# A 1 MB load cut into 8 runs and 24 runs in a kernel whose DMA engines are always busy

## The chip, the cores and the metric

The kernel runs on one core of a Trainium2 chip. A core has five engines that run their own instruction streams: PE (matrix products), ACT and DVE (element-wise work), POOL, and SP, which here only issues transfers. Sixteen DMA engines move data between the device memory and the core's 128-partition memory. The metric is the device time of one execution in microseconds; the runs of the kernel before have a median of 323.83 us.

## The reference

`x` is 128 batches of 128 channels by 1024 time steps in float32 (67.1 MB). Each batch has a subject number, which picks one of eight 128 x 128 weight matrices. The output is `x` plus the product of the picked matrix, transposed, with `x`:

```python
w = weights[subjects]
out = jnp.einsum('bct,bcd->bdt', x, w)
x = x + out
```

All of `x` is read once and an output of the same size is written once.

## The kernel before

A tile is four batches, 2 MB. There are 32 tiles (`NT`), and 12 slots (`SLOTS`) of 16 KB a partition hold them; tile i lies in slot i mod 12. The result replaces the input in its slot and is stored from there.

*Loads.* `load` (L142) issues two transfers of 1 MB for a tile, both on ACT's queue, one for each pair of batches (`H` = 2 pairs of `G` = 2). A transfer reads 32 runs of eight rows, 32 KB each and contiguous in device memory, and puts two rows into each of 128 partitions, so a run fills four partitions with 8 KB each: the first batch of a pair lies in partitions 0 to 63, the second in 64 to 127. Each transfer adds 16 to the semaphore `s_in` of its tile's place modulo 4 when it is complete. Four tiles (`AHEAD`) are loaded ahead before anything else on ACT (L263). After that ACT's loop (L268) waits for a tile (`landed`, L154: 32 on its semaphore), waits for a free slot (`s_empty`, which POOL raises as stores complete), issues the load four tiles on, and then calls `trade` for the tile that has landed.

*Trade.* Two halves of partitions are exchanged by five copies on ACT (`move`, L152), so that each batch has its two rows of a channel pair where the product needs them. `trade` ends with `s_ready`.

*Product.* For each pair, DVE places four weight matrices with the identity added (`place`, L192), so that the product contains the `+ x`; PE multiplies them with the slot's rows in pieces of 512 columns (L204); DVE copies the result from the accumulators into the slot (L216) and raises `s_added`. Before the first tile DVE and POOL rearrange the eight weight matrices, and eight dummy products run on PE.

*Stores.* SP waits for `s_added` and issues stores: the first 20 tiles one by one with 2 MB each, the last 12 in pairs of 4 MB. The first one is issued at L306, the others through `transfer` (L66), which ACT's loads use too. The program ends when the last store has landed.

## Time and profile before

| | |
|---|---|
| runs, median (lowest to highest) | 323.83 us (323.4 to 324.35) |
| profiled execution, its own time | 323.66 us |
| its span, first to last instruction | 321.7 us |
| bytes read, written | 67.63 MB, 67.11 MB |
| mean rate over the span | 419 GB/s |
| PE, ACT, DVE busy | 77%, 61%, 56% |
| loads of x: number, size, median to landing | 64, 1024 KB, 11.6 us |
| stores of 2 MB: number, median to landing | 20, 52.1 us |
| stores of 4 MB: number, median to landing | 6, 32.3 us |

The page cuts the span into 40 slices of 8 us. A digit is the busy share in tenths, and the DMA row is the mean of the 16 DMA engines. A DMA queue is a list of transfers of one issuing engine; both queues are worked on by the same 16 engines. A packet is what one engine moves in one piece, or the small write by which it reports that its part is complete. Packets are counted in the stretch in which they start, so that a short stretch can show a share above 1. In a row of windows the columns are the stretch, its length, busy time and count of instructions of PE, its weight loads, DVE, ACT and POOL, then the clock that PE was granted, the DMA share and GB/s.

### The profile page before, as it was taken

What the parts mean: (1) busy time and instruction counts of PE and PEld (TensorE: products, weight loads), DVE (VectorE), ACT (ScalarE), POOL (GpSimd) and SP (SyncE); (2) the same over time, 40 slices, a digit from 0 to 9 for tenths busy, and PEclk for the clock granted to TensorE, in tenths of its full rate; (3) what the DMA queues carried; (4) which work ended last, traced back from release to release, by engine and by line L of the source; (5) the groups of instructions that cost most, each with busy time, mean ns of one, the idle gap of its engine ahead of it and who ended that gap; (6) DMA issues with size and microseconds to landing.
All of it is one profiled execution on the core that took longest, in us unless ns stands there. A gap on an engine that the chain in (4) does not pass through costs nothing. (4 is left out here: it accounts for less than half of the span.)

```text
span 321.7 us, 2843 instructions
## 1 busy us (share of the span) xinstructions
PE 247.7 (77%) x528; PEld 102.2 (32%) x528; DVE 181.4 (56%) x217; ACT 195.7 (61%) x162; POOL 2.5 (1%) x10
## 2 busy tenths in 40 slices
PE   7479987888888888888793998749787589999200
PEld 3134332333333333333341433313333234444000
DVE  3707765666666665666275276544743666677500
ACT  1577767776777677775627766377662799990000
POOL 0200000000000000000000000000000000000000
PEclk9969999999999999999798699998997999999955
DMA  8999999999999999999999999999999999999994
GB/s 318 399 456 440 401 418 403 432 438 432 424 454 403 436 418 442 436 436 426 405 428 434 424 420 438 418 434 434 416 442 418 448 405 432 428 434 432 428 428 200
DMA packets 7731, 134.76 MB, mean 419 GB/s; under 512 B 1457, under 2 KB 1458, under 8 KB 2098
## 3 DMA queue, kind: packets, MB, share of 16 engines
q1 hardware_dynamic: 4658, 67.64, 49.7%
q10 hardware_dynamic: 3072, 67.11, 48.9%
q14 instruction: 1, 0.01, 0.0%
HBM read 67.63 MB, written 67.11 MB: 419 GB/s over the span
## 5 line engine op out<-in xcount | busy, mean ns | idle before, releaser
L204 PE MATMUL ps<-x_all,w 128*128 x512 | 237.5, 618 | 50.1 <-PEq L200 49.5
L216 DVE COPY x_all<-ps 128x2048 f32 x64 | 146.7, 2292 | 114.8 <-DVEq L215 114.8
L204 PEld LDWEIGHTS ps<-x_all,w 128*128 128x128 f32 x512 | 98.2, 197 | 189.5 <-issue 189.5
L152 ACT COPY aside<-x_all 64x1024 f32 (+1 forms) x64 | 66.7, 1042 | 76.9 <-issue 75.1
L152 ACT COPY x_all<-aside 64x1024 f32 (+1 forms) x64 | 66.8, 1044 | 4.7
L152 ACT COPY x_all<-x_all (+1 forms) x32 | 60.7, 1897 | 6.2 <-ACTq L162 5.7
L192 DVE TENSOR_TENSOR w<-w_all,eye 128x128 f32<-128x128 f32 x132 | 31.8, 283 | 0.8 <-issue 0.8
L228 PE MATMUL ps<-x_all 128*128 128x512 f32 x16 | 10.2, 808 | 1.7 <-DVE x_all L225 1.7
L228 PEld LDWEIGHTS ps<-x_all 128*128 128x128 f32 x16 | 4.1, 262 | 7.0 <-issue 5.3
L266 ACT ACT_TABLE_LOAD x1 | 1.3, 1283 | 6.2 <-issue 6.2
L286 DVE COPY w_all<-x_all 32x256 f32<-32x256 f32 x12 | 3.9, 327 | 0.4
L237 DVE STREAM_TRANSPOSE x_all<-x_all 128x512 f32<-128x512 f32 x2 | 2.0, 1082 | 3.0 <-DMA x_all<-in_L_cond_weights_dram 3.0
L286 POOL COPY w_all<-x_all 32x256 f32<-32x256 f32 x4 | 1.7, 427 | 7.0 <-DVE x_all L283 6.8
L283 DVE STREAM_TRANSPOSE x_all<-x_all 128x1024 f32<-128x1024 f32 x1 | 1.2, 1225 | 0.0
L225 DVE MEMSET x_all<- 128x512 f32 x1 | 0.5, 485 | 1.0 <-SPq L218 1.0
L243 DVE TENSOR_SCALAR x_all<-x_all 1x128 int32<-1x128 int32 x1 | 0.2, 215 | 0.7 <-DMA x_all<-in_itok_B_dram 0.7
L253 POOL TENSOR_SCALAR_AFFINE_SELECT eye<-x_all 128x128 f32<-128x128 f32 x1 | 0.3, 294 | 1.4 <-DVE x_all L225 1.4
L247 DVE CUSTOM_DVE_ANT_0 index<-x_all 1x256 uint16<-1x256 uint16 x1 | 0.3, 280 | 0.0
L253 POOL TENSOR_SCALAR_AFFINE_SELECT eye<-eye 128x128 f32<-128x128 f32 x1 | 0.3, 294 | 0.1
L245 DVE TENSOR_SCALAR x_all<-x_all 1x128 int32<-1x128 int32 x1 | 0.2, 216 | 0.0
L266 ACT COPY mark<-eye 1x1 f32<-1x1 f32 x1 | 0.2, 190 | 0.0
L353 POOL MEMSET const-bfloat16-1.0<- 128x1 bf16 x1 | 0.1, 101 | 0.0
(5 smaller groups left out, 0.4 us busy)
## 6 DMA issues: line engine op xcount, KB each, us to landing
x_all<-in_x_dram ACTq DMA_DIRECT2D x64, 1024.0 KB, 11.6
out_dram<-x_all SPq DMA_DIRECT2D x20, 2048.0 KB, 52.1
out_dram<-x_all SPq DMA_DIRECT2D x6, 4096.0 KB, 32.3
x_all<-in_L_cond_weights_dram SPq DMA_DIRECT2D x1, 512.0 KB, 3.7
x_all<-in_itok_B_dram SPq DMA_DIRECT2D x1, 0.5 KB
```

The source lines that it names most:

```text
L152: return nc.scalar.copy(out, in_)
L192: copy = nc.vector.tensor_tensor(ws[q], w_all[:, bass.ds(subject[q], 1), :], eye, ALU.add)
L204: mm = nc.tensor.matmul(ps[h][:, q % G, t : t + N], ws[q][:, 0, :], x_all[:, bass.ds(at, N)], start=True, stop=True,)
L216: nc.vector.tensor_copy(mine, ps[h].rearrange("d g t -> d (g t)")).then_inc(s_added, 1)
L225: nc.vector.memset(zeros, 0.0).then_inc(s_zeros, 1)
L228: nc.tensor.matmul(ps[P_SLOTS - 1][:, G - 1, :N], zeros[:, :D], zeros, start=True, stop=True)
L237: nc.vector.transpose(w_mid.rearrange("p (e r h w j) -> p r j h e w", e=4, r=R, h=4, w=8)[:, r], w_raw.rearrange("p (j r d) -> p r j d", r ...
L247: nc.vector.tensor_tensor(index[:, :B], near, wrap, ALU.add).then_inc(s_index, 1)
L253: nc.gpsimd.affine_select(eye[:, 0], eye[:, 0] if r else zeros[:, :D], [[-1, D]], ALU.not_equal, 1.0, base=r - r * R * A, channel_multipli ...
L266: nc.scalar.copy(mark, eye[:1, 0, :1]).then_inc(s_moved, H)
L283: nc.vector.transpose(w_late, w_mid).then_inc(s_sort, 1)
L286: engine.tensor_copy(w_all[32 * v : 32 * (v + 1), 2 * o : 2 * (o + 1), :], w_late[32 * o : 32 * (o + 1)].rearrange("c (e u r d) -> c u r e ...
```

## The change

The second transfer of tile 0, batches 2 and 3 into slot 0, is issued as two transfers: first the last 8 of its 32 runs, into partitions 96 to 127, then the other 24, into partitions 0 to 95. The first of them reports to a semaphore of its own, `s_cut`; the second to `s_in[0]` as before. ACT waits for `s_cut` once, ahead of its loop. All other loads are issued as before.

```diff
+CUT = 24
...
+    s_cut = tc.alloc_semaphore("s_cut")
...
-    def load(k, slot, first):
+    def load(k, slot, first, cut=None):
         for h in range(H):
-            transfer(
-                nc,
-                nc.scalar,
-                x_all[:, bass.ds(slot * (H * G * T) + h * G * T, G * T)],
-                x[bass.ds(first + h * G, G)].rearrange("h (b r) t -> (h b) (r t)", r=ROWS),
-            ).then_inc(s_in[k], DMA)
+            there = x_all[:, bass.ds(slot * (H * G * T) + h * G * T, G * T)]
+            runs = x[bass.ds(first + h * G, G)].rearrange("h (b r) t -> (h b) (r t)", r=ROWS)
+            if cut and h:
+                rows = cut * ROWS // R
+                transfer(nc, nc.scalar, there[rows:], runs[cut:]).then_inc(s_cut, DMA)
+                there, runs = there[:rows], runs[:cut]
+            transfer(nc, nc.scalar, there, runs).then_inc(s_in[k], DMA)
...
         for i in range(AHEAD):
-            load(i % AHEAD, i, i * (H * G))
+            load(i % AHEAD, i, i * (H * G), None if i else CUT)
         nc.scalar.wait_ge(s_eye, R)
         nc.scalar.copy(mark, eye[:1, 0, :1]).then_inc(s_moved, H)
         nc.gpsimd.wait_ge(s_eye, R).then_inc(s_empty, SLOTS - 1 - AHEAD)
+        nc.scalar.wait_ge(s_cut, DMA)
         with nc.scalar.Fori(0, NT // AHEAD - 1) as turn:
```

## The prediction

> **What bounds the kernel now.** I read the page's slices first, because 134.76 MB pass through one core and the busiest compute engine is idle for a quarter of the span:

> ```profile
> PE 247.7 (77%) x528; PEld 102.2 (32%) x528; DVE 181.4 (56%) x217; ACT 195.7 (61%) x162; POOL 2.5 (1%) x10
> DMA  8999999999999999999999999999999999999994
> DMA packets 7731, 134.76 MB, mean 419 GB/s; under 512 B 1457, under 2 KB 1458, under 8 KB 2098
> q1 hardware_dynamic: 4658, 67.64, 49.7%
> q10 hardware_dynamic: 3072, 67.11, 48.9%
> ```

> The 16 DMA engines are busy in every slice but the first and the last, and the two queues (q10 holds the loads, q1 the stores and the two small inputs) add up to 98.6% of 16 engines' span. No compute engine comes near that. Next the view of SP's waits and the windows, for the middle and for the end:

> ```profile
> SPq L362 <- DMA out_dram<-x_all: 17.4, 1, 17.4
> 60.00:300.00 240.00, 200.36 (x432) 82.72 (x432) 145.33 (x163) 158.33 (x131) 0.00 (x0) 0.96 1.01 429
> 302.50:316.00 13.50, 0.00 (x0) 0.00 (x0) 0.00 (x0) 0.00 (x0) 0.00 (x0) 0.59 1.00 427
> ```

> From 60 to 300 us the DMA share is 1.01 (packets are counted where they start) at 429 GB/s, and after 302.5 nothing computes: the rest is stores draining, and the program's end waits 17.4 us for them. The chain of waits stops at the last compute work and does not show this tail. So the time is the time of the DMA engine that ends last, and the question is which engine that is and how much work it has. The DMA view of four short stretches at the end answers the first half (each fence line is that stretch's count; stretches 316.0 to 317.0, 317.0 to 318.7, 318.7 to 319.5, 319.5 to 321.7):

> ```profile
> DMA packets 16, 0.52 MB, mean 524 GB/s; under 512 B 0, under 2 KB 0, under 8 KB 0
> ...
> DMA packets 16, 0.07 MB, mean 39 GB/s; under 512 B 14, under 2 KB 14, under 8 KB 14
> ...
> DMA packets 2, 0.03 MB, mean 41 GB/s; under 512 B 1, under 2 KB 1, under 8 KB 1
> ...
> DMA packets 1, 0.00 MB, mean 0 GB/s; under 512 B 1, under 2 KB 1, under 8 KB 1
> ```

> The packets under 512 B are completion marks, one for each engine of a transfer (the count is checked below). Fourteen engines post the mark of the last store before 318.7, one between 318.7 and 319.5, and the last one after 319.5: it started its final 32 KB piece in the third stretch, alone. One engine thus ends about 2 us behind the bulk of the others, although by packets all 16 have had the same bytes. The page does not say which of the 16 it is.

> **The change part by part.**

> (1) *Work by engine.* q10 has 3072 packets for 64 loads, 48 each: 32 runs of 32 KB and 16 marks. Check: 64 and 26 transfers of 16 marks, 16 for the weights and one for the 512 B of indices are 1024 + 416 + 16 + 1 = 1457, the number under 512 B. So a load of 32 runs occupies 16 engines with two runs each, and a transfer of one run occupies one engine. The time of a run on its engine is 48.9% of 321.7 us x 16 engines / 2048 runs = 1.23 us. For the 8 runs and the 24 runs no row exists. The bounds: if the chip cut both pieces evenly over all 16 engines, every engine would keep its 64 KB and this part is 0; if the pieces are dealt in whole runs and begin at the same engine, some engines get 3 runs where they had 2, others 0. I take the second, because the rows (32 runs to 16 engines, one run to one) fit whole runs dealt over as many engines as divide their number, which is 8 engines with one run each and then 12 with two each: 8 engines get three runs (+1.23 us), 4 keep two (0), 4 get none (-2.46 us).

> [...]

> (2) *Is the added work covered?* Nothing hides it. All engines have queued work from the first load to the end: reads alone move at 430 GB/s and then mixed traffic keeps the share of 1.01, so an engine with 1.23 us more work early ends 1.23 us later, and one with less ends earlier.

> ```profile
> 6.84:9.28 2.44, 2.44 (x6) 1.10 (x5) 1.83 (x4) 0.84 (x2) 0.00 (x0) 1.00 1.00 430
> 9.28:11.72 2.44, 2.44 (x6) 0.78 (x5) 2.25 (x7) 0.17 (x1) 1.71 (x4) 1.00 1.00 430
> ```

> Whether the time follows depends on whether the engine that ends last is one of the 8. By count alone that is 8 in 16. But if it is among the 4 unchanged or the 4 relieved, the 8 heavier ones of the other fifteen still end 1.23 us later, so a relief wins little (below). I take it among the 8.

> (3) *Sharing of partitions.* [...] If the way into a group of partitions is no wider than one engine, two engines that meet there halve. Bounds: 0, and all three shifted runs of a heavy engine at half speed, 3 x 1.23 = 3.7 us. No row shows two engines on one group. I take one run's worth, 1.2 us, since runs that collide drift apart as soon as one engine is ahead.

> [...]

> (4) *Two more instructions on ACT.* One more DMA issue, and a wait on the 8 runs ahead of the loop. In the rows of the order below (ACT's start, with the two pieces as 32 and 96 partitions) the loads sit ahead of everything else on ACT.

> ```order
> L66 DMA x_all<-in_x_dram 128x2048 x8
> L266 ACT_TABLE_LOAD [waits s_eye]
> L266 COPY mark<-eye 1x1
> L268 UNCONDITIONAL_BRANCH
> L64 ISA [waits s_in0,s_empty]
> ```

> ```order
> L68 DMA x_all<-in_x_dram 128x2048
> L68 DMA x_all<-in_x_dram 32x2048
> L68 DMA x_all<-in_x_dram 96x2048
> L68 DMA x_all<-in_x_dram 128x2048 x6
> L270 ACT_TABLE_LOAD [waits s_eye]
> L270 COPY mark<-eye 1x1
> L273 UNCONDITIONAL_BRANCH [waits s_cut]
> L66 ISA [waits s_in0,s_empty]
> ```

> Eight transfers became nine, with the new wait in front of the loop that already waits for slot 0. The timeline of ACT prices it:

> ```profile
> 0.90 5.21 ACTq L66 DMA_DIRECT2D x_all<-in_x_dram  x8
> 6.20 1.28 ACT L266 ACT_TABLE_LOAD   x1 [6.20 <-issue]
> 7.50 0.19 ACT L266 COPY mark<-eye 1x1 f32<-1x1 f32 x1
> 10.22 1.16 ACTq L66 DMA_DIRECT2D x_all<-in_x_dram  x2
> 11.55 2.11 ACT L152 COPY aside<-x_all 64x1024 f32 x2 [3.86 <-issue]
> 18.45 1.15 ACTq L66 DMA_DIRECT2D x_all<-in_x_dram  x2
> 26.66 1.15 ACTq L66 DMA_DIRECT2D x_all<-in_x_dram  x2
> ```

> An issue takes 5.21 / 8 = 0.65 us; it lies in the gap between 7.69, when the mark is made, and 10.22, when slot 0 has landed. The queue stays full, for a load takes 2.44 us to move and 0.65 to issue. Cost 0. The new wait adds nothing to the wait for slot 0; behind it stand the issues of slot 4 and the first copies of slot 0.

> (5) *Slot 0 lands later*, by what the heavy engines lose, 2.4 us. ACT's loop and with it PE, DVE and the first store move by that. The cover is the read queue: at 10.22 three slots are still to come, three times 4.88 us, and each later turn brings a slot of 4.88 us after 8.2 us until the first stores join. At 26.66 + 2.4 the load of slot 6 is issued; slots 1 to 5 keep the engines busy until 9.8 + 5 x 4.88 = 34 (slot 0 was there shortly before 10.22). Cost 0; without that cover it would be the whole 2.4 us once more. ACT's 75.1 us of waiting through the loop take up the shift of the compute chain.

> *Sum* against the profiled execution: 323.66 + 1.23 + 1.2 + 0 + 0 = 326.1. Its span is 321.7, with 2.0 us around it; the three runs have 323.83 as median, 0.2 above it. The forecast's own range, with sharing from 0 to 2.5 us, is 324.9 to 327.4.

> **The rivals.**

> *Relief (faster).* The engine that ends last is one of the four that lose two runs; it then ends 2.46 us sooner, before the bulk. From there the heavy engines decide: their marks come between 317.0 and 318.7 and move to 319.9 at most without sharing, against a last mark that now comes 1.23 us after a start in 318.7 to 319.5, between 319.9 and 320.7. Its price is a gain of 0 to 1 us, about 0.5: 323.2. The point from which it decides is a lag of the last engine over the bulk larger than 1.23 us, which holds; against it: only 4 engines in 16, and any sharing eats it. [...]

> *Full sharing.* The heavy engines' three shifted runs all go at half speed: 323.66 + 1.23 + 3.7 = 328.6. For it: an engine's rate is the same 26.9 GB/s in reads and mixed traffic, as if something one engine wide set it. Against: the collisions need both engines in step for three runs.

> *No effect.* The chip spreads both pieces over all engines, or the last engine is one of the four unchanged and nothing is shared: 323.7. For it: the mean load is unchanged. Against: 32 KB runs appear whole in the counts.

> **How the numbers follow.** Forecast 0.62 (326.1), full sharing 0.10, relief 0.14, no effect 0.14. A measurement here tells about 0.3%, 1 us, from no change. Faster by more than that: only the best part of the relief, 0.07. Within: the rest of relief (0.07), no effect (0.14) and a sliver of the forecast's low end, 0.23 together. Slower: 0.70. The range 323.0 to 327.7 leaves out most of the full sharing and the best of the relief.

> **What would show it.** In the changed profile q10 should have 3072 + 4 = 3076 packets (8 + 8 and 24 + 12 in place of 48); 3088 would mean 16 engines for each piece and no effect. In the stretches at the end more than two engines should post their last mark late, or the last one later than 319.5 by 1.2 to 3.7 us. Slot 4's issue on ACT should move from 10.22 by 1.2 to 5. Wrong it would be if the last mark comes earlier while q10 has 3076 packets (relief), or if the DMA share drops below 0.9 somewhere between 30 and 60 us, which would mean that the cover of part 5 failed.

## The result, and the profile after

| | before | after |
|---|---|---|
| median of the runs (lowest to highest) | 323.92 us (323.4 to 324.35) | 328.35 us (327.99 to 328.57) |
| profiled execution, its own time | 323.66 us | 328.3 us |
| its span | 321.7 us | 326.4 us |

The change makes the kernel slower by 4.4 us, a ratio of 1.014 (1.0127 to 1.0152). The forecast was 326.1 with a range of 323.0 to 327.7: the direction is right, the time lies 0.65 us above the range.

The page after, its line of all packets and the two queues:

```profile
DMA packets 7735, 134.76 MB, mean 413 GB/s; under 512 B 1461, under 2 KB 1462, under 8 KB 2102
q10 hardware_dynamic: 3076, 67.11, 49.3%
q1 hardware_dynamic: 4658, 67.64, 49.0%
```

The loads have 3076 packets and the same bytes as before. Their time is 49.3% of 326.4 us, 160.9 us for each engine, against 48.9% of 321.7 = 157.3 before: 3.6 us more for the same bytes. The stores' time is unchanged, 49.0% of 326.4 = 159.9 against 49.7% of 321.7 = 159.9. So the time went into the loads, and the windows show where. First the kernel before, then the kernel after, in the same four stretches from the moment when the changed transfers begin:

```profile
6.40:10.00 3.60, 3.60 (x8) 1.37 (x8) 2.74 (x8) 1.28 (x2) 0.57 (x2) 1.00 1.00 428
10.00:17.60 7.60, 1.85 (x5) 0.54 (x3) 4.20 (x15) 5.70 (x5) 1.14 (x3) 0.81 1.08 466
17.60:28.00 10.40, 9.58 (x18) 4.09 (x19) 3.42 (x4) 6.45 (x7) 0.00 (x0) 0.81 0.97 416
28.00:36.00 8.00, 7.36 (x18) 3.13 (x17) 6.19 (x7) 6.06 (x5) 0.00 (x0) 1.00 0.99 417
```

```profile
6.40:10.00 3.60, 3.60 (x9) 1.55 (x9) 2.77 (x9) 1.47 (x2) 0.64 (x2) 1.00 1.43 282
10.00:17.60 7.60, 1.19 (x3) 0.19 (x1) 4.15 (x14) 0.62 (x1) 1.06 (x3) 0.72 0.84 276
17.60:28.00 10.40, 4.21 (x6) 1.88 (x7) 0.00 (x0) 8.03 (x8) 0.00 (x0) 0.55 1.04 447
28.00:36.00 8.00, 7.94 (x19) 3.33 (x18) 5.38 (x6) 5.57 (x5) 0.00 (x0) 1.00 0.94 401
```

The last two columns give the mean time of one 32 KB run on its engine: share x 16 engines x 32.77 KB / rate, or share x 524.3 / rate. Before it is 1.22 us in each of the first three stretches (1.00 x 524.3 / 428, 1.08 x 524.3 / 466, 0.97 x 524.3 / 416). After it is 2.66 us from 6.4 to 10, 1.60 to 17.6, and from there 1.22 again. The engines are busy all the time, but a run takes 2.2 times as long in the first of them. By rate x length the four rows before hold 12.74 MB, those after 10.97; the missing 1.77 MB are 4.1 us at 430 GB/s.

(Packets are counted where they start, so a stretch of 3.6 us is exact to about a run.)

The records of the single packets say how many engines that concerns. This table takes the 32 KB runs in the order of their start, sixteen at a time, which is one round of the 16 engines; it is counted from the trace:

```
        before                                    after
round   starts (us)     shortest  mean  longest   starts (us)     shortest  mean  longest
2        5.07 to  5.82    1.21    1.25   1.37      5.05 to  5.53    1.21    1.23   1.30
3        6.30 to  7.04    1.21    1.24   1.38      6.33 to  6.75    2.00    2.63   3.12
4        7.65 to  8.25    1.21    1.22   1.25      8.33 to  9.56    2.48    2.62   2.90
5        8.86 to  9.47    1.21    1.21   1.21     11.23 to 12.05    2.28    2.30   2.31
6       10.07 to 10.68    1.21    1.21   1.21     13.54 to 14.34    1.50    1.62   1.93
7       11.29 to 11.89    1.21    1.21   1.22     15.46 to 15.83    1.22    1.22   1.22
```

Rounds 1 and 2 are slot 0's first load, untouched. From the third on four rounds are slow in a row after the change, and all sixteen runs of each are: the shortest of rounds 4 and 5 take 2.48 and 2.28 us. The excess over 1.216 us, the usual time of a run, of all runs that start before 40 us is 4.4 us for each engine, before it is 0.2: a stall of 4.2 us, in agreement with the missing bytes. Below, "stall" is this excess with the 0.2 taken off, from the profiled execution of each kernel.

The start of ACT moves by it. ACT's timeline after (start, length, what):

```profile
0.91 6.61 ACTq L68 DMA_DIRECT2D x_all<-in_x_dram  x9
7.61 1.28 ACT L270 ACT_TABLE_LOAD   x1 [7.61 <-issue]
8.90 0.19 ACT L270 COPY mark<-eye 1x1 f32<-1x1 f32 x1
15.65 1.16 ACTq L68 DMA_DIRECT2D x_all<-in_x_dram  x2
```

Nine issues take 6.61 us, 0.73 each. Slot 4's load, issued when slot 0 has landed and at 10.22 before, is issued at 15.65: 5.4 us later. A loaded engine has three slow rounds to do for slot 0 (2.63 + 2.62 + 2.30) where it had two of 1.22; that makes 5.1 of it. That later start costs nothing of its own, as the windows from 30 to 60 and from 60 to 300 us show:

```profile
30.00:60.00 30.00, 25.97 (x59) 10.69 (x58) 20.90 (x24) 20.45 (x18) 0.00 (x0) 1.00 1.01 431
60.00:300.00 240.00, 199.48 (x429) 82.30 (x427) 142.60 (x159) 163.25 (x135) 0.00 (x0) 0.95 1.01 429
```

The engines never run dry. At the end all is later by the same amount. The DMA view after, in three stretches from 316 to 321, to 323.5 and to 326:

```profile
DMA packets 64, 2.10 MB, mean 419 GB/s; under 512 B 0, under 2 KB 0, under 8 KB 0
...
DMA packets 24, 0.29 MB, mean 118 GB/s; under 512 B 15, under 2 KB 15, under 8 KB 15
...
DMA packets 2, 0.03 MB, mean 13 GB/s; under 512 B 1, under 2 KB 1, under 8 KB 1
```

Fifteen marks of the last store (the packets under 512 B) come between 321 and 323.5, the last one alone after 323.5, at 324.97. Before, the last one came at 320.36: 4.6 us. By the packet records the sixteen marks now fall into two groups: eight come from 321.36 to 321.52 and eight from 322.26 on. Before, fourteen came within 0.9 us.

### The profile page after: what moved, and what is told of

The parts are those of the page before. It is cut to its first block, busy times and chain, and to the rows that moved or that the text cites. A ratio compares the mean times of both kernels' runs of the same rounds, so it can differ in the third digit from the quotient of the medians.

```text
span 326.4 us, 2844 instructions
## 1 busy us (share of the span) xinstructions
PE 248.3 (76%) x528; PEld 102.6 (31%) x528; DVE 181.4 (56%) x217; ACT 195.7 (60%) x162; POOL 2.5 (1%) x10
## 2 busy tenths in 40 slices
DMA  8999999999999999999999999999999999999994
DMA packets 7735, 134.76 MB, mean 413 GB/s; under 512 B 1461, under 2 KB 1462, under 8 KB 2102
## 3 DMA queue, kind: packets, MB, share of 16 engines
q10 hardware_dynamic: 3076, 67.11, 49.3%
q1 hardware_dynamic: 4658, 67.64, 49.0%
HBM read 67.63 MB, written 67.11 MB: 413 GB/s over the span
## 5 line engine op out<-in xcount | busy, mean ns | idle before, releaser
L232 PE MATMUL ps<-x_all 128*128 128x512 f32 x16 | 9.5, 761 | 1.7 <-DVE x_all L229 1.7
L270 ACT COPY mark<-eye 1x1 f32<-1x1 f32 x1 | 0.2, 191 | 0.0
```

Of the source, the lines that this page charges most:

```text
L232: nc.tensor.matmul(ps[P_SLOTS - 1][:, G - 1, :N], zeros[:, :D], zeros, start=True, stop=True)
L270: nc.scalar.copy(mark, eye[:1, 0, :1]).then_inc(s_moved, H)
```

## The experiments

The theories. *Collision*: engines that write at the same time through the same way into the partitions slow each other, and that makes up the stall. It supposes that an engine writes the same partitions in every whole load, its "own"; the packet records name no engine, so no run shows that, and "own" and "others'" are words of this theory. *Work*: the third run of eight engines is what counts, collisions are small. *Issue*: the extra transfer, its semaphore and ACT's wait delay the start. Each kernel was timed beside the kernel before on the same chip; "+" is the difference of the two medians. The expectations call the collision theory sharing, stall or meeting theory too, and the work theory deal theory.

### One extra transfer of 8 runs, at its engines' own place or at others'

Both kernels leave all loads whole and add one transfer of 8 runs behind slot 0's first load, with the semaphore and the wait of the change. It reads runs that are loaded anyway and puts them into slot 5, which is overwritten later by its own load: 0.26 MB more are read, and the output is unchanged. One writes partitions 0 to 31, which by the collision theory belong in a whole load to the eight engines that get the 8 runs; the other writes 96 to 127, as the change does, where by the same theory other engines are writing.

```diff
+            if cut and h:
+                there2 = x_all[0:32, bass.ds(5 * (H * G * T), G * T)]
+                transfer(nc, nc.scalar, there2, runs[cut:]).then_inc(s_cut, DMA)
             transfer(nc, nc.scalar, there, runs).then_inc(s_in[k], DMA)
```

> The kernel before, with one transfer more behind the first load of slot 0: 8 runs of x are also read into partitions 0 to 31 of slot 5, which its own load later overwrites. Eight engines get one run more; partitions 0 to 31 are taken to be the ones that these engines write in a full load. Sharing theory (a transfer is slow where its engines write partitions that other engines write at the same time): no slow runs, all runs near 1.22 us, and the time is that of one run at most, 323.9 to 325.2. Deal theory (only the number of runs on an engine counts): the same, 325.1. Issue theory (any additional transfer and wait ahead of the loop costs what the change cost): 328.3.

> As the run with 8 more runs, but into partitions 96 to 127 of slot 5. The engines' work is the same run for run. Sharing theory: runs of 2 us and more around 6 to 9 us, loads of slot 0 and 1 late by 1 to 3 us, and 325.5 to 328. Deal theory: 325.1, no difference from partitions 0 to 31. Issue theory: 328.3.

Measured, own partitions: 325.12 us (8 runs, 325.04 to 325.5), +1.04, ratio 1.0029 (1.0018 to 1.004). Other engines' partitions: 325.07, 325.45, 325.74, 325.97 and 328.76, the median +1.66, ratio 1.0046 (1.0029 to 1.0063). The windows, own and then other, the latter of the execution of 328.76:

```profile
6.40:10.00 3.60, 3.60 (x8) 1.51 (x8) 2.97 (x9) 1.47 (x2) 0.83 (x2) 1.00 1.03 437
10.00:17.60 7.60, 1.57 (x4) 0.38 (x2) 3.96 (x14) 4.76 (x4) 0.86 (x3) 0.77 1.07 461
```

```profile
6.40:10.00 3.60, 3.60 (x10) 1.52 (x8) 3.01 (x10) 1.47 (x2) 1.06 (x3) 1.00 0.91 273
10.00:17.60 7.60, 0.49 (x2) 0.00 (x0) 3.70 (x13) 3.64 (x3) 0.64 (x2) 0.85 1.03 397
17.60:28.00 10.40, 7.44 (x12) 3.28 (x13) 0.95 (x1) 8.11 (x8) 0.00 (x0) 0.62 1.04 400
```

With their own partitions a run takes 1.24 and 1.22 us, as before, and the kernel pays 1.04 us. That fits the extra run of eight engines. By these times alone it could also be the 0.26 MB more, 0.6 us at 430 GB/s, because the interval of the ratio reaches from 0.6 to 1.3 us; the ends of the engines, below, speak for the run. With others' partitions a run takes 1.75 us in the first stretch. The difference between the kernels is only where the 8 runs are written, so the place makes the stall, not the extra run or the extra transfer. In this execution a run then stays at 1.36 us (1.03 x 524.3 / 397, 1.04 x 524.3 / 400), long after the 8 runs are done. That was not in any theory.

The same kernel was timed and profiled once more:

> The 8 more runs into partitions 96 to 127 once more, for a second profile and more times. In the first profile the runs stayed at 1.36 us from 9 us to 36 us, after the collision was over, and that execution took 328.76 where the others took 325.1 to 326. If that state comes by chance: a profile with either 1.22 or 1.36 us after the collision, and times near 325.5 without it and near 328.5 with it. If the profile alone makes it: again 1.36 and 328.5 in the profiled execution.

Measured: seven executions at 325.26 to 325.77, and two at 329.25 and 329.35. The profiled one has 325.46:

```profile
6.40:10.00 3.60, 3.60 (x8) 1.46 (x8) 2.48 (x8) 1.47 (x2) 0.36 (x1) 1.00 1.01 291
10.00:17.60 7.60, 1.74 (x5) 0.43 (x3) 4.46 (x15) 3.42 (x3) 1.34 (x4) 0.79 1.09 466
```

A run takes 1.82 us at first and 1.23 from 10 us on. So the price of the collision of these 8 runs is a stall of 1.1 us here, and the long tail at 1.36 us is a second thing that some executions have and others do not, 3.6 us apart in their times. The 1.1 us and the run of 1.04 make 2.1; the profiled execution is +1.5, so about 0.6 comes back elsewhere.

### The second load cut evenly, and cut by columns

Cut at 16 runs, each piece goes to all 16 engines, one run each (a transfer of 16 runs had 16 marks where transfers ran alone, from 18 to 20.5 us in the last kernel below), and no engine gets more work; but each piece puts 16 engines into only 64 partitions. Cut by columns (all first rows of each partition's two, then all second rows), each piece covers all 128 partitions in 4 KB pieces, with the same extra issue, semaphore and wait. Both diffs are against the kernel after.

```diff
-CUT = 24
+CUT = 16
```

```diff
             if cut and h:
-                rows = cut * ROWS // R
-                transfer(nc, nc.scalar, there[rows:], runs[cut:]).then_inc(s_cut, DMA)
-                there, runs = there[:rows], runs[:cut]
+                pairs = x[bass.ds(first + h * G, G)].rearrange("h (p u) t -> (h p) u t", u=R)
+                transfer(nc, nc.scalar, there[:, T:], pairs[:, 1]).then_inc(s_cut, DMA)
+                there, runs = there[:, :T], pairs[:, 0]
```

> The cut at 16 in place of 24: the second load of slot 0 as 16 runs into partitions 64 to 127 and 16 runs into 0 to 63. By whole runs each piece gives one run to each of 16 engines, so that all engines have the work of before. Deal theory: 323.9. Sharing theory: each piece has 16 engines on half of the partitions, so its 1.22 us become about 2.44 each, at least 2.4 us in all: 326.3 to 328. Issue theory: 328.3.

> The second load of slot 0 is also issued as two transfers with the same semaphores and wait, but each covers all 128 partitions with half the bytes (the odd rows first, then the even rows, 4 KB pieces). Sharing theory and deal theory: every engine keeps its bytes and its partitions, 323.9 within 0.5. Issue theory: 328.3.

Measured, evenly: 325.89 us (325.53 to 326.23), +1.8, ratio 1.0053 (1.0036 to 1.007). By columns: 324.39 (10 runs, 323.83 to 325.14), +0.3, ratio 1.0012 (0.9999 to 1.0025). The windows, evenly and then by columns:

```profile
6.40:10.00 3.60, 3.60 (x10) 1.52 (x8) 2.52 (x8) 1.47 (x2) 0.41 (x1) 1.00 0.97 246
10.00:17.60 7.60, 0.58 (x2) 0.00 (x0) 4.41 (x15) 3.98 (x3) 1.29 (x4) 0.86 0.99 410
```

```profile
6.40:10.00 3.60, 3.60 (x9) 1.50 (x9) 2.58 (x8) 1.47 (x2) 0.62 (x2) 1.00 1.20 426
10.00:17.60 7.60, 1.31 (x4) 0.24 (x2) 4.16 (x14) 5.20 (x5) 1.07 (x3) 0.74 0.97 418
```

The even cut has no imbalance and still stalls: 2.07 us for a run in the first stretch, a stall of 1.8 us in all, and that is its whole loss. It is less than the 326.3 to 328 that the collision theory had named, which took each run at half speed, and the work theory's 323.9 is missed as well. By columns 426 GB/s are moved while the cut load runs, and from 10 us on 32 KB take 1.22 us (0.97 x 524.3 / 418); no 32 KB run takes longer than before. The small pieces themselves are not free: by the packet records the sixteen pieces of 4 KB of an engine take 3.2 us together, where its two runs took 2.4, and the rounds behind them start 0.8 us later than before. In the median +0.3 us is left of that, which cannot be told from nothing. The extra issue, its semaphore and the wait are in this kernel too, so they cost no more than that.

### The order of the pieces, the place of the 8 runs, and both loads cut

Three variants of the change itself. One issues the 24 runs first, then the 8. One cuts at the other end: runs 0 to 7, into partitions 0 to 31, go first, then the other 24 into 32 to 127, so that by the collision theory the 8 runs collide with nobody and only the 24 are shifted. One cuts both loads of slot 0 at 24.

```diff
+                transfer(nc, nc.scalar, there[:rows], runs[:cut]).then_inc(s_cut, DMA)
+                there, runs = there[rows:], runs[cut:]
```

```diff
+                first_runs = H * 16 - cut
+                rows = first_runs * ROWS // R
+                transfer(nc, nc.scalar, there[:rows], runs[:first_runs]).then_inc(s_cut, DMA)
+                there, runs = there[rows:], runs[first_runs:]
```

```diff
-            if cut and h:
+            if cut:
...
-        nc.scalar.wait_ge(s_cut, DMA)
+        nc.scalar.wait_ge(s_cut, DMA * H)
```

> The change with its two pieces in the other order: the 24 runs first, then the 8. Stall theory (while engines write partitions that are not theirs in a full load, all 16 engines slow down): the same runs of 2 to 3 us from 6 us on, for about as long, 327 to 329. Deal theory with sharing only between the two engines that meet: 326 to 327.5, and the four engines without a run in either piece keep 1.22 us in most runs.

> The change with the 8 runs taken from the front: runs 0 to 7 into partitions 0 to 31 (which cost nothing but their own run in the run with 8 more), then the other 24 into partitions 32 to 127. The engines get the same numbers of runs as in the change. Stall theory: the 8 runs are free of it and the 24 are not; slow runs begin about 1 us later and last less, 326.5 to 328. If the 8 runs alone made the stall: 325.1.

> Both loads of slot 0 are cut at 24, and the wait ahead of the loop is for both first pieces. Stall theory: the stretch of slow runs is twice as long, about 18 us, and the loss is twice 4.4, 332 to 333.5. Deal theory (one run more on 8 engines per cut, the rest once only): 329.5 to 330.

Measured: swapped 327.35, 327.55, 327.58, 327.59 and 330.3, ratio 1.0111 (1.0094 to 1.0128); 8 runs at their own place 326.96, 327.14, 327.22 and 330.4, ratio 1.0132 (1.0077 to 1.0187); both loads cut 332.12 (332.06 to 332.16), ratio 1.0253 (1.0236 to 1.0271). The windows of the profiled executions: swapped (the one of 330.3), own place (327.22), both cut:

```profile
6.40:10.00 3.60, 3.60 (x10) 1.52 (x8) 2.76 (x8) 1.47 (x2) 0.61 (x2) 1.00 1.15 273
17.60:28.00 10.40, 5.05 (x6) 2.19 (x7) 0.00 (x0) 8.05 (x7) 0.00 (x0) 0.50 1.01 388
```

```profile
6.40:10.00 3.60, 3.60 (x8) 1.50 (x8) 3.23 (x9) 1.47 (x2) 0.71 (x2) 1.00 1.09 291
10.00:17.60 7.60, 1.70 (x4) 0.39 (x3) 4.09 (x14) 1.50 (x2) 0.99 (x3) 0.79 1.01 345
```

```profile
6.40:10.00 3.60, 3.60 (x9) 1.50 (x9) 3.40 (x10) 0.98 (x1) 1.30 (x3) 1.00 1.12 228
10.00:17.60 7.60, 1.31 (x4) 0.24 (x2) 3.45 (x13) 0.49 (x2) 0.40 (x1) 0.74 0.94 207
```

With the 8 runs at their own place a run takes 1.96 and then 1.54 us; the stall is 2.9, all of it from the 24 runs. The extra transfer alone gave 1.1 for 8 runs in 96 to 127. Together they make 4.0, against 4.2 in the change, as if the two pieces' stalls added up (the 24 runs lie in 32 to 127 here and in 0 to 95 there, so this is no proof). With both loads cut a run takes 2.58 and then 2.38 us, the stall is 6.4, and the loss 8.2 us, 1.84 times that of one cut (332.12 - 323.95 against 4.43). The order of the pieces matters little: the swapped kernel is +3.6 in four of five executions, 0.8 less than the change, and its profiled one has the long tail (1.01 x 524.3 / 388 = 1.36 us from 17.6 to 28). By the packet records all sixteen runs of two rounds in a row take 2.33 to 2.38 us there, also those of the four engines that get no run of either piece; sharing between two engines that meet would have left these at 1.22 us in most runs, by the expectation.

The end of the kernel with the 8 runs at their own place shows how the work lies on the engines. The DMA view in the stretches 316 to 319, 319 to 321, 321 to 323.5 and 323.5 to 326:

```profile
DMA packets 40, 1.18 MB, mean 393 GB/s; under 512 B 4, under 2 KB 4, under 8 KB 4
...
DMA packets 17, 0.43 MB, mean 213 GB/s; under 512 B 4, under 2 KB 4, under 8 KB 4
...
DMA packets 9, 0.07 MB, mean 26 GB/s; under 512 B 7, under 2 KB 7, under 8 KB 7
...
DMA packets 1, 0.00 MB, mean 0 GB/s; under 512 B 1, under 2 KB 1, under 8 KB 1
```

Four engines post the mark of the last store from 318.16 to 318.37, four from 320.05 to 320.32, and eight from 321.19 on, the last one at 323.88 (times by the packet records). That is the division into four engines with no run, four with two and eight with three, and the engine that ends last is one of the eight. With both loads cut the marks come in the same groups of 4, 4 and 8: to 323.09, from 324.58 to 324.81, and from 326.18 on.

### Four runs instead of eight

Three kernels add a transfer of 4 runs to whole loads, again redundant reads into slot 5: into partitions 0 to 15 (by the theory the own place of the engines that take them), into 112 to 127, and into 96 to 111. The first also asks which engine ends last: if it is one of those that take the extra runs, the kernel pays 1.04 us again, and if not, nothing. The third asks whether the long tail comes with 112 to 127 alone.

```diff
+                there2 = x_all[0:16, bass.ds(5 * (H * G * T), G * T)]
+                transfer(nc, nc.scalar, there2, runs[32 - 4:]).then_inc(s_cut, DMA)
```

> [...] No slow runs. [...]

> Four more runs in place of eight, into partitions 112 to 127 of slot 5, beside the loads as in the run with 8. Stall theory with a price by the runs that collide: half of the stall of 8 runs, 0.55 us for each engine in place of 1.1, and slow runs on all 16 engines again; 324.5 to 325.7 and, if the 1.36 us state comes, 3 us more in that execution. If any collision costs the same: 1.1 us, 325.5.

> [...] If the lasting state comes from which engines meet: no 1.46 us after 10 us, and about 324.5 to 325. If it comes from any four runs in foreign partitions: 1.46 us again until the first store, and 328.3 to 330.

Measured: 0 to 15, 324.15 us (10 runs, 323.7 to 324.53), ratio 1.0005 (0.9995 to 1.0016); 112 to 127, 328.34, 328.35, 329.15 and 330.0, ratio 1.0148 (1.0118 to 1.0178); 96 to 111, six executions at 324.89 to 325.25 and three at 327.86, 329.16 and 329.32, ratio 1.0077 (1.0037 to 1.0117). Windows, in this order (the third of the execution of 324.89):

```profile
10.00:17.60 7.60, 0.43 (x1) 0.00 (x0) 3.96 (x14) 4.72 (x4) 0.87 (x3) 0.84 1.09 470
```

```profile
6.40:10.00 3.60, 3.60 (x10) 1.57 (x9) 3.02 (x9) 1.47 (x2) 0.91 (x2) 1.00 1.02 309
10.00:17.60 7.60, 0.96 (x3) 0.14 (x1) 3.85 (x14) 3.39 (x3) 0.80 (x2) 0.91 1.07 384
17.60:28.00 10.40, 7.19 (x10) 3.09 (x11) 0.34 (x1) 8.11 (x8) 0.00 (x0) 0.57 0.98 353
```

```profile
6.40:10.00 3.60, 3.60 (x10) 1.56 (x9) 2.94 (x9) 1.47 (x2) 0.82 (x2) 1.00 1.11 355
10.00:17.60 7.60, 0.70 (x2) 0.00 (x0) 3.96 (x14) 3.84 (x3) 0.88 (x3) 0.88 1.05 448
```

The 4 runs at their own place cost nothing that can be measured (+0.2). Eight cost 1.04. The engine that ends last is one of the eight, as the marks above show. Were it one of those that take these 4 runs, the 1.04 would come again, and the interval ends at 0.5. So it is none of them; which engines take them no run shows. The 4 runs at 112 to 127 missed their expectation of 324.5 to 325.7 by 3 us, since all four executions lie in the range that the long tail gives elsewhere in these kernels; in the profiled one a run stays at 1.46 us (1.07 x 524.3 / 384 and 0.98 x 524.3 / 353). The 4 runs at 96 to 111 settle at 1.23 us in the profiled execution and leave +1.0 in two of three executions. In that execution, too, all sixteen runs of the first slow round take 1.68 to 2.28 us and all of the second 1.38 to 1.77, by the packet records, although by the collision theory four extra runs meet only some of the other engines at a time. Neither of the two expectations for 96 to 111 holds as it stands: the long tail comes with these partitions too, but not in every execution.

### The collision without other traffic

Two kernels run transfers alone, behind the weights and ahead of all loads, while ACT waits, so that the loads start late and the total time is of no use. The first moves only the 8 runs into 96 to 127. The second moves three pairs of transfers: runs 0 to 7 and 8 to 15 into partitions 0 to 31 and 32 to 63; runs 24 to 31 and 16 to 23 into 96 to 127 and 64 to 95, both on eight engines; and twice the 16 runs of partitions 64 to 127, on all 16 engines, each of which has four partitions for itself. All of it is redundant reading into slots that their own loads fill later. `alone` issues one such transfer; its numbers are the first run, the number of runs and the slot.

```diff
+        alone(0, 8, 5)
+        alone(8, 8, 5)
+        nc.scalar.wait_ge(s_cut, 2 * DMA)
+        alone(24, 8, 5)
+        alone(16, 8, 5)
+        nc.scalar.wait_ge(s_cut, 4 * DMA)
+        alone(16, 16, 6)
+        alone(16, 16, 7)
+        nc.scalar.wait_ge(s_cut, 6 * DMA)
```

> The 8 more runs into partitions 96 to 127 are issued alone: ACT waits for the weights, issues them, waits until they have landed, and only then issues the loads of x. So the start is late by about 8 us, which is not what is looked at. Stall theory (it takes other engines writing those partitions at the same time): each of the 8 runs takes 1.22 us. If runs into partitions of other engines are slow by themselves: 2 us or more.

> [...] The start is late by some 15 us, which is not what is looked at. Of each pair the second run of an engine counts. Meeting theory: 1.22, 1.22 and 2.4 us. Foreign partitions slow by themselves: 1.22, 1.8 or more, 1.8 or more. If only a mixture with full loads is slow: 1.22 three times.

The first kernel (331.25 us, one execution) told nothing: its 8 runs show, from 5 to 8 us,

```profile
q10 hardware_dynamic: 14, 0.26, 30.4%
```

30.4% x 16 x 3 us / 8 = 1.82 us each, but in the same kernel the first runs of the whole loads, where nothing collides, took up to 2.07 us when the engines started from idle. Hence the pairs in the second kernel (344.82 us, one execution), whose second transfers start on busy engines. The DMA view of the second transfer of the pair that starts with 96 to 127, into 64 to 95 (13 to 14.2 us), and of the second one with 16 engines in 64 partitions (19 to 20 us):

```profile
DMA packets 16, 0.26 MB, mean 218 GB/s; under 512 B 8, under 2 KB 8, under 8 KB 8
q10 hardware_dynamic: 16, 0.26, 50.8%
...
DMA packets 30, 0.49 MB, mean 492 GB/s; under 512 B 15, under 2 KB 15, under 8 KB 15
q10 hardware_dynamic: 30, 0.49, 233.0%
```

## Why the prediction was wrong

**Part (1), the work by engine, held.** The loads have the 3076 packets that it named. One more run on eight engines without a collision cost 1.04 us, against 1.23 taken. The groups of 4, 4 and 8 marks in the kernel with the 8 runs at their own place are the division that it took. The 4 packets added are marks, 8 + 12 in place of 16, so 8 and 12 engines; which of the 16 they are no run shows.

**Part (2), no cover and a last engine among the eight, held.** 8 extra runs without a collision cost 1.04 us, and the last mark is one of the group of eight in the kernel with the 8 runs at their own place. That it would be among the eight was a choice with 8 in 16 for it by count, so this part was right in part by luck.

**Part (3), the sharing of partitions, is the step that failed**, by its size: 1.2 us taken, 4.2 measured, above its upper bound of 3.7. Half speed was right where transfers ran alone: sixteen engines in 64 partitions take 2.47 in place of 1.21 us. Wrong was who pays and for how long. The prediction let only heavy engines pay, for three runs, and then took one run because "runs that collide drift apart". In the trace all 16 engines pay, for four rounds in a row (means of 2.63, 2.62, 2.30 and 1.62 us), and they do not drift apart: the sixteen starts of a round stay within 0.4 to 1.2 us. What the sum lacked is that the other engines are held up too. No run shows its term of 1.2 us, nor that engines meet at each other's partitions. In its place the runs show a stall of 4.2 us on all 16 engines, and that the partitions count: 8 extra runs into 0 to 31 left a run at 1.24 us from 6.4 to 10, the same runs into 96 to 127 made it 1.75 and 1.82 in the two profiled executions; alone, 8 engines in 32 partitions took 1.22 us, 16 engines in 64 took 2.47.

**Part (4), issue and wait, held**: the cut by columns has them and its small pieces besides, and is +0.3 with an interval that touches no change.

**Part (5), the cover for the late slot 0, held.** Slot 4 was issued 5.4 us later, more than the 1.2 to 5 named, because the stall was larger; from 30 to 60 us the share was 1.01 and the rate 431 GB/s.

**The sum with measured terms** is 323.66 + 1.04 + 4.2 = 328.9, against 328.3 of the profiled execution. The 0.6 too much appears in the queue's time too: the loads' 3.6 us more for each engine are 0.6 less than the stall. From 30 to 60 us the kernel after moves 431 GB/s; the same stretch before reads:

```profile
30.00:60.00 30.00, 25.60 (x58) 10.39 (x56) 19.10 (x22) 21.77 (x19) 0.00 (x0) 1.00 0.99 413
```

18 GB/s over 30 us are 0.54 MB, 1.3 us at 430 GB/s. So some of the loss may be regained there, when the first stores join the loads. But the even cut, which has no extra run, loses 1.6 us in its profiled execution for a stall of 1.8, while the kernels that have an extra run and a stall lose 0.3 to 0.7 us less than the two together. So the two do not simply add; why was not settled.

**The rivals.** *Relief* is out: the last engine is among the loaded ones. *No effect* is out by the packets and the time. *Full sharing* (its 26.9 GB/s are the windows' 430 / 16) gave 328.6, 0.25 from the median, and had the right kind of cause, but not the right account: it had only the heavy engines at half speed for three runs, and it is the shorter stall of all engines plus the extra run that comes to the same number. It was held down to 0.10 by the argument that engines would have to stay in step, and the trace shows that they do.

No version tried was faster than the kernel before. If the second load must be cut, the cut by columns, over all partitions, is the cheapest of those tried (+0.3, not to be told from nothing).

## What to carry to other kernels

When the DMA engines are the bound, look at which partitions each transfer writes: two transfers over 32 and 96 partitions, next to loads in flight, made a stall of 4.2 us here, four times their extra work of 1.04; 8 runs into 96 to 127 made one of 1.1, and 8 into 0 to 31 none that a window shows. Price such a stall with all 16 engines, as it was here, not with those that meet, and read the mean time of a run off a windows row as share x 16 x run size / rate: a share near 1 does not mean a full rate (0.97 with 246 GB/s in the even cut, 1.00 with 428 before). The one split of a load here without that price had each piece cover all partitions; its price was that of smaller pieces, 0.8 us at the start and +0.3 in the time.

## What the runs showed that was not expected

**A collision beside running loads slows all 16 engines.** After the change it is all runs of four rounds, 1.50 to 3.12 us each, and with no more than 4 extra runs into 96 to 111 all runs of two rounds, 1.38 to 2.28, against 1.21 before. Alone, with all 16 engines in 64 partitions, it is a plain halving, 2.46 to 2.48 us. What makes all 16 slow beside running loads was not tested.

**The stall can leave a lasting state.** In some executions all runs stay at 1.36 us (8 extra runs into other engines' partitions, and the swapped order) or 1.46 us (4 runs into 112 to 127) from 10 to 15 us on, until the first store joins at 37 to 40 us. It costs some 3 to 4 us. By the times it was there in 1 of 5 and 2 of 9 executions of the 8 extra runs, 1 of 5 with the swapped order, 1 of 4 with the 8 at their own place, 3 of 9 with 4 runs into 96 to 111, and 4 of 4 with those into 112 to 127; only three of these were seen in a profile. It was in no execution of the kernels before and after, of the even cut and the cut by columns, of the double cut, and of the extra runs at their own place. What decides it stays open.

**One engine ends 1.5 us behind all others**, before (320.36 against 318.87 for the next) and after (324.97 against 323.36). By the marks it is one of the eight that the change loads, and by the +0.2 of the four extra runs into 0 to 15 none of those that take them; why it lags was not tested. The four engines that the change relieves lost 2.4 us of work. In the kernel with the 8 runs at their own place four engines end 1.9 us before the next four. In the changed kernel they do not: relieved and unchanged engines together make up the eight marks from 321.36 to 321.52. Why was not settled.
